# A two-layer graph-attention kernel: another order of the pieces where one batch hands over to the next, and edge masks loaded ahead of the source row

## The chip, the cores and the metric

The kernel runs on one core of a Trainium2 chip. The metric is the time of one launch on the device, in microseconds (us). A core has five engines with a queue of instructions each: TensorE (PE in the profile: matrix products; its weight loads are shown apart as PEld), VectorE (DVE), ScalarE (ACT), GpSimd (POOL) and SyncE (SP, which here only starts DMA transfers). They run side by side and wait for each other through semaphores.

## What is computed

x has 8 batches of 2048 nodes with 256 features; adj is a 2048 x 2048 mask of 0 and 1. Layer 0 is attention in four heads of 64, with a softmax of its own in each chunk of 256 keys, and layer 1 is a graph attention with additive scores. Each layer's output is added to its input and normalized. Cut to what matters:

```python
# layer 0
q, k, v = heads(x @ Wq.T + bq), heads(x @ Wk.T + bk), heads(x @ Wv.T + bv)
s = clip(q @ k.T / 8, -10, 10);  s = where(adj == 0, -10, s)
ctx = sum over chunks j of softmax(s[:, chunk j]) @ v[chunk j]
o = layernorm(ctx @ Wo.T + bo + x) * gamma + beta
x = layernorm(x + o)
# layer 1
Wh = x @ W
e = leaky_relu(s_src[:, None] + s_dst[None, :], 0.2), masked by adj
x = layernorm(x + elu(softmax(e) @ Wh))
```

## The kernel before

All 16 node tiles of 128 of one batch stay on the chip: `qT`, `kT` (features on the partitions), `vaug` (values and a column of ones, which gives the softmax sums) and `h1` (the output of layer 1). The 2048 query nodes are cut into four groups of 512, g = 0 to 3.

The order of each engine's instructions is the order in which the program writes them: scheduling is manual. The main loop over batches `b` has 64 slots `s`. A slot computes the scores of the next 512 queries by 256 keys for two heads (`scores`, L361), clips and masks them on VectorE (L382), takes exps on ScalarE (L394) and multiplies by the values (`product`, L396). `normalize` (L415) divides on GpSimd and adds to `acc`. Beside it runs layer 1 of the batch before (class `Layer1`): `make` (L689) builds a masked weight tile `e` on VectorE (L702) from a broadcast source row `srow`, a factor `gd` and the edge mask `et`, and `use` (L713) multiplies it by `waug` (L722). `tile_pool` buffers and PSUM tiles are handed on by semaphores; `two_banks` (L102) alternates between two PSUM tiles of two banks each, so a group of matmuls waits until the group two before it in that alternation was evicted.

Each 512-query group of layer 0 must, after its contexts are complete, go through: the output product (`Between.output`, L512), the add with x (L530), a norm (`a`), gamma and beta, a second add and norm (`b2`), the store of x1 (L546), a transposition, and the product with W (`values`, L554), whose results are the node values `waug` and the scores `sd` for layer 1. For groups 0 to 2 this is spread over the slots of the following group (tables `AHEAD`, `BESIDE`, `BEHIND`, `AFTER`). Group 3 has no slots after it. Its pieces are done between the last slot of one batch and the first slot of the next. With them go:

- the projections of the next batch, cut into pieces by `project` (L296): for each group g, `l` loads x, `t` transposes it on VectorE (L281), `k`, `v` and `q` are TensorE products (L315, L331) followed by an eviction on ScalarE (L323, L338). The piece `q3` takes PSUM tiles of another pool, and `l0` and `t0` are done earlier;
- `ctx`, the transposition of the last group's second half of contexts on TensorE (L454, evicted at L457), which needs the `acc` that GpSimd has just finished;
- `steps`, group 3's way to layer 1: 0 bias, 1 output product, 2 add, 3 shift and statistics of the first norm, 4 apply the first norm, 5 scale, second add and its statistics, 6 apply the second norm and store, 7 transposition of the eight blocks of y (`turn_all`, L290, evicted at L293), 8 and 9 the products with W (L565);
- `fs`, the three steps of `factors` (L604): the maximum of the destination scores, its spread with the exps, and the row: a transposed copy is stored to `rowD` in DRAM (L646) and scales `waug` on GpSimd (L649);
- `rest`, pieces of the closing work of layer 1's last unit (L744 to L758).

The list `order` in the program (L965 to L980) says in which order these pieces are written, and so fixes every engine's queue there. After it `Layer1(b, gd, waug)` is built, which issues the first loads on SyncE: the row (L673), which must come back from DRAM after the store at L646, and two edge tiles (L684), which come from masks stored at the start.

Of the kernel before, what the change touches and what calls it, by code (L numbers as in the profile page):

```python
# [22 lines left out]
def adj_resnorm_kernel(  # L23
# [170 lines left out]
    def send():  # L194
        while outgoing:
            outgoing.pop(0)()


    class Masks:
# [3 lines left out]
        def __init__(self):  # L203
            self.pieces = [(t, m) for t in range(NT) for m in range(len(BANKS))]
            self.raw, self.bits, self.done = [], [], []
            self.next = 0
# [148 lines left out]
    def load_slab(s):  # L355
        q, hp, c = where[s]
        slab = slabs.tile([P, KT, CH], I8, tag="slab", name="slab")
        nc.sync.dma_start(out=slab, in_=clipD[q][:, KT * c : KT * (c + 1), :])
        slab_of[s] = slab

    def scores(s):  # L361
        q, hp, c = where[s]
        slab = slab_of.pop(s)
        cols = slice(q * CH, (q + 1) * CH)
        pss = []
        for u in range(KT):
            t = KT * c + u
            ps = two_banks([P, 2, CH], "ps")
            for k in range(2):
                rows = slice(k * D, (k + 1) * D)  # L370
                nc.tensor.matmul(  # L371
                    ps[:, k, :],
                    lhsT=kT[rows, hp, t * P : (t + 1) * P],
                    rhs=qT[rows, hp, cols],
                    start=True,
                    stop=True,
                )
            pss.append(ps)
        probs[s] = []
        for u in range(KT):  # L380
            pr = prp.tile([P, 2, CH], F32, tag="pr", name="pr")
            nc.vector.scalar_tensor_tensor(  # L382
                pr,
                pss[u],
                -CLIP,
                slab[:, u, :].unsqueeze(1).to_broadcast([P, 2, CH]),
                op0=ALU.max,
                op1=ALU.min,
            )
            probs[s].append(pr)  # L390

    def exps(s, u):
        pr = probs[s][u]
        nc.scalar.activation(pr, pr, AF.Exp, scale=0.125)  # L394
# [46 lines left out]
    def load_context(b, q, hp):  # L441
        t = small.tile([P, 1, CH], F32, tag="ctx", name="ctx", bufs=1)
        load_squares(t, ctxD[b, q * CH : (q + 1) * CH, hp * P : (hp + 1) * P])
        sums[q, hp] = t

    def turn_context(q, hp):

        nc.vector.transpose(qT[:, hp, q * CH : (q + 1) * CH], sums.pop((q, hp))[:, 0, :])  # L448
# [209 lines left out]
    class Layer1:  # L658
        def __init__(self, b, gd, waug):
            self.b, self.gd, self.waug = b, gd, waug  # L660
            self.made = self.used = 0
            self.rows, self.edge, self.e = {}, {}, {}
            self.tail = []
            self.load_row(0)
            self.load_edge(0)
            self.load_edge(1)

        def load_row(self, n):
            if n < len(UNITS):
                m, h = UNITS[n]  # L670
                srow = small.tile([P, WIDE * P], F32, tag="srow", name="srow")
                i0, w = FIRST[m] * P, BANKS[m] * P
                nc.sync.dma_start(  # L673
                    out=srow[:, :w], in_=rowD[self.b, h, i0 : i0 + w].partition_broadcast(P)
                )
                self.rows[n] = srow
# [190 lines left out]
    for b in range(B):  # L867
        waug = blocks.tile([P, NT, H, D1], F32, tag="waug", name="waug")
        sd = small.tile([P, 2 * H, NT], F32, tag="sd", name="sd", bufs=1)
        if b == 0:  # L870
            for s in range(3):
                load_slab(s)
            scores(0)
            for u in range(KT):
                exps(0, u)
        if lower:
            for _ in range(STEP):
                lower.make()
        closing = Closing(b - 2, CLOSING) if b > 1 else None
        if closing:  # L880
            closing.do(-1)
        group = None
        for s in range(SLOTS):
            q, hp, c = where[s]
            i = s % QS
            send()
            if s + 3 < SLOTS:
                load_slab(s + 3)
            if i == 0:
                before = group  # L890
                group = Between(b, q - 1, sd, waug) if q else None
            if i == 1 and q:
                load_context(b, q - 1, 1)
            if i == QS // 2 + 1:
                load_context(b, q, 0)
            if group and i in AHEAD:
                AHEAD[i](group)
            if s == SLOTS - 3 and b + 1 < B:
                turns = [project(b + 1, g) for g in range(NCH)]
                turns[0].pop(0)()  # L900
            if s:
                normalize(s - 1)
            if s + 1 < SLOTS:
                scores(s + 1)

            if s == SLOTS - 1 and b + 1 < B:
                turns[0].pop(0)()
            if i == 3 and q:
                turn_context(q - 1, 1)
            if i == QS // 2 + 3:  # L910
                turn_context(q, 0)
            if group:
                for step in BESIDE.get(i, ()):
                    step(group)
            elif closing:
                closing.do(s, behind=False)
            product(s, 0, not lower)
            if s + 1 < SLOTS:
                for u in range(KT):
                    exps(s + 1, u)  # L920
            if lower:
                if b + 1 < B or s < SLOTS - LATE:
                    lower.step()
            elif masks.left():
                masks.step()
            product(s, 1, not lower)

            if before and i in AFTER:
                AFTER[i](before)
            if i == 0 and q:  # L930
                send_context(b, q - 1, 1)
            if i == QS // 2:
                send_context(b, q, 0)
            if group and i in BEHIND:
                BEHIND[i](group)
            elif closing and not q:
                closing.do(s, beside=False)
        normalize(SLOTS - 1)

        send()  # L940
        before = group
        gd, fs = factors(b, sd, waug)
        group = None
        every = tuple(range(QT))

        def begin():
            nonlocal group
            group = Between(b, NCH - 1, sd, waug)

        def ctx():  # L950
            context(NCH - 1, 1)

        steps = [
            lambda: group.bias(),
            lambda: group.output(every),
            lambda: group.add(every),
            lambda: (group.shift(), group.a.stats(every)),
            lambda: group.a.apply(group.y),
            lambda: (group.scale(), group.again(), group.b2.stats(every)),
            lambda: group.finish(),  # L960
            lambda: group.turn_all(),
            lambda: group.values((0, 1)),
            lambda: group.values((2, 3)),
        ]
        if b + 1 < B:  # L965
            (k0, v0, q0), (l1, t1, k1, v1, q1), (l2, t2, k2, v2, q2), (l3, t3, k3, v3, q3) = turns
            rest = [lambda: lower.rest(1)] if lower else []
            order = [begin, *rest, l1, *rest, lambda: before.values((2, 3)), *rest, k0, *rest, ctx]
            order += [v0, steps[0], t1, steps[1], k1, steps[2], q0, *steps[3:5], l2, v1, steps[5]]
            order += [steps[6], t2, q1, l3, k2, *steps[7:10], v2, fs[0], t3, q2, fs[1]]  # L970
            order += [lambda: [load_slab(s) for s in range(3)], k3, fs[2], v3]
            order += [lambda: scores(0), q3, lambda: [exps(0, u) for u in range(KT)]]
        else:

            step = lower.step
            order = [begin, lambda: before.values((2, 3)), steps[0], step, ctx, step, steps[1], step]
            order += [steps[2], step, steps[3], step, steps[4], step, steps[5], step, steps[6], step]
            order += [steps[7], step, steps[8], step, steps[9], step, fs[0], step, fs[1], step, fs[2]]
            order += [step, lambda: lower.rest(4)]
            assert sum(p is step for p in order) == LATE  # L980
        for piece in order:
            send()
            piece()
        send()
        lower = Layer1(b, gd, waug)
# [56 lines left out]
```

## Time and profile before

The median of 3 launches is 3862.64 us (3862.37 to 3863.09). The profiled launch spans 3861.0 us.

| Engine | Busy, us | Share of the span |
|---|---|---|
| TensorE, matrix products | 3687.8 | 96% |
| VectorE | 3204.6 | 83% |
| TensorE, weight loads | 2746.0 | 71% |
| ScalarE | 1953.6 | 51% |
| GpSimd | 1387.4 | 36% |

The mean granted clock of TensorE is 0.991 of full speed. A row of the page's groups names the line, the engine, the operation and its tiles, how often it ran, its busy time and mean duration, and the idle time of its engine just ahead of it with the releaser that ended most of it. In a timeline a row is one instruction or a run of like ones: start, duration, engine, line, operation, and in brackets the idle time ahead of it and what ended it. In a table of stretches each row has the length of the stretch, the busy time of each engine with its count of instructions, the granted TensorE clock, the DMA share and the GB/s moved.

### The profile page before, as it was taken

The numbers are of one execution on the slowest core, as the hardware profiler recorded it, in microseconds if no ns is written. First come the engines' busy times: TensorE is split into PE (matmuls) and PEld (weight loads), VectorE is DVE, ScalarE is ACT, GpSimd is POOL, SyncE is SP. The second block draws the span as 40 slices with busy tenths as digits, with TensorE's granted clock in tenths as the row PEclk, the third lists the DMA queues.
The fourth block names the chain that finished last, engine by engine and source line by source line (L and its number), as shares of the span: only waits on it lengthen the run. The fifth ranks groups of instructions, "written<-read, shape, count | busy, mean of one in ns | idle before, by whom it ended". The sixth has DMA issues, their size and how long they took to land. (4 is left out here: it accounts for less than half of the span.)

```text
span 3861.0 us, 160222 instructions
## 1 busy us (share of the span) xinstructions
PE 3687.8 (96%) x72068; PEld 2746.0 (71%) x72068; DVE 3204.6 (83%) x4810; ACT 1953.6 (51%) x3601; POOL 1387.4 (36%) x1202
## 2 busy tenths in 40 slices
PE   7999999999999999999999999999999999999787
PEld 4656677776777777776777767777677777776676
DVE  3877499986999779995999959998699977998798
ACT  3666445554555555554555545555455555555321
POOL 0445233332433333433433324343243333344310
PEclk9999999999999999999999999999999999999999
DMA  7642333333433333333433334333343433333344
GB/s 148 154 109 62 83 101 96 97 89 98 112 101 100 80 121 102 102 94 73 140 96 100 99 87 135 96 98 87 103 111 99 103 80 118 102 102 86 92 147 123
DMA packets 771328, 398.48 MB, mean 103 GB/s; under 512 B 442576, under 2 KB 735824, under 8 KB 770640
## 3 DMA queue, kind: packets, MB, share of 16 engines
q1 hardware_dynamic: 720640, 354.54, 36.3%
q10 hardware_dynamic: 50000, 33.70, 2.7%
q8 instruction: 563, 9.22, 1.0%
q14 instruction: 125, 1.02, 0.1%
HBM read 331.22 MB, written 56.89 MB: 101 GB/s over the span
## 5 line engine op out<-in xcount | busy, mean ns | idle before, releaser
L382 DVE SCALAR_TENSOR_TENSOR pr<-ps,slab 128x1024 f32<-128x1024 f32 x1024 | 1192.1, 1205 | 208.8 <-PE ps L371 206.7
L702 DVE SCALAR_TENSOR_TENSOR e<-srow,gd,et 128x640 f32<-128x640 f32 (+1 forms) x1536 | 1349.6, 934 | 17.9 <-DMA et<-edgeD 12.5
L406 PEld LDWEIGHTS pc<-vaug,pr 128*64 128x64 f32 x32768 | 1040.6, 138 | 445.5 <-issue 245.3
L406 PE MATMUL pc<-vaug,pr 128*64 128x65 f32 x32768 | 1157.9, 224 | 42.6 <-ACT raw L413 35.1
L394 ACT ACTIVATE pr<-pr 128x1024 f32<-128x1024 f32 x1024 | 1053.0, 1058 | 184.5 <-DVE pr L382 168.4
L722 PE MATMUL pa<-waug,e 128*64 128x65 f32 x32768 | 1081.5, 224 | 42.4 <-DVE e L702 40.0
L722 PEld LDWEIGHTS pa<-waug,e 128*64 128x64 f32 x32768 | 1020.1, 139 | 68.1 <-DVE e L702 39.8
L371 PE MATMUL ps<-qT,kT 64*128 64x512 f32 x4096 | 1027.4, 619 | 6.8 <-DVE pr L382 6.5
L428 POOL TENSOR_TENSOR part<-raw,rd 128x512 f32<-128x512 f32 x448 | 469.5, 1048 | 1462.1 <-DVE rd L421 1449.7
L413 ACT COPY raw<-pc 128x260 f32<-128x260 f32 x1024 | 384.9, 376 | 1157.7 <-PE pc L406 1132.2
L430 POOL TENSOR_TENSOR acc<-acc,part 128x512 f32<-128x512 f32 x448 | 574.9, 1283 | 35.1
L371 PEld LDWEIGHTS ps<-qT,kT 64*128 64x128 f32 x4096 | 351.3, 186 | 330.4 <-issue 209.7
L421 DVE RECIPROCAL rd<-raw 128x8 f32<-128x8 f32 x512 | 101.1, 197 | 116.7 <-ACT raw L413 113.0
L428 POOL TENSOR_TENSOR acc<-raw,rd 128x512 f32<-128x512 f32 x64 | 66.9, 1045 | 352.8 <-DVE rd L421 352.0
L750 ACT ACTIVATE hh<-pa,dn 128x64 f32<-128x64 f32 x512 | 114.4, 320 | 100.7 <-DVE dn L746 96.9
L315 PE MATMUL pp<-xT,wk_sb 128*128 128x512 f32 x256 | 124.1, 630 | 36.9 <-DVE xT L281 36.9
L565 PE MATMUL pw<-w_sb,x1T 128*128 128x264 f32 x512 | 138.7, 406 | 17.0 <-ACT x1T L293 9.0
L481 POOL TENSOR_TENSOR rs_c<-rs_c,nhalf 128x4 f32<-128x4 f32 x32 | 55.6, 1738 | 226.9 <-DVE off_c L480 226.9
L521 PE MATMUL po<-wo_sb,qT 128*128 128x256 f32 x512 | 125.5, 389 | 2.1 <-DVE qT L448 1.5
L315 PEld LDWEIGHTS pp<-xT,wk_sb 128*128 128x128 f32 x256 | 49.8, 200 | 94.3 <-issue 73.1
L315 PE MATMUL pp<-xT,wq_sb 128*128 128x512 f32 x256 | 116.0, 596 | 0.0
L331 PE MATMUL pv<-wv_sb,xT 128*128 128x256 f32 x512 | 115.9, 379 | 0.0
(90 smaller groups left out, 1885.1 us busy)
## 6 DMA issues: line engine op xcount, KB each, us to landing
et<-edgeD SPq DMA_DIRECT2D x256, 320.0 KB, 3.2
slab<-clipD SPq DMA_DIRECT2D x512, 128.0 KB, 3.6
et<-edgeD SPq DMA_DIRECT2D x128, 384.0 KB, 3.5
srow<-rowD SPq DMA_DIRECT2D x64, 320.0 KB, 4.4
xp<-in_x_dram SPq DMA_DIRECT2D x256, 64.0 KB, 2.3
xg<-in_x_dram SPq DMA_DIRECT2D x32, 512.0 KB, 4.7
x1D<-y ACTq DMA_DIRECT2D x32, 512.0 KB, 3.1
x1g<-x1D SPq DMA_DIRECT2D x32, 512.0 KB, 5.7
```

The lines of the kernel that those rows point to most:

```text
L315: nc.tensor.matmul(pps[c], lhsT=w[:, kc, c * P : (c + 1) * P], rhs=st["xT"][:, kc, :], start=(kc == 0), stop=(kc == KC - 1),)
L371: nc.tensor.matmul(ps[:, k, :], lhsT=kT[rows, hp, t * P : (t + 1) * P], rhs=qT[rows, hp, cols], start=True, stop=True,)
L382: nc.vector.scalar_tensor_tensor(pr, pss[u], -CLIP, slab[:, u, :].unsqueeze(1).to_broadcast([P, 2, CH]), op0=ALU.max, op1=ALU.min,)
L394: nc.scalar.activation(pr, pr, AF.Exp, scale=0.125)
L406: nc.tensor.matmul(pc[z * D : (z + 1) * D, i, :], lhsT=probs[s][u][:, k, i * P + z * D : i * P + (z + 1) * D], rhs=vaug[:, KT * c + u, 2 * ...
L413: nc.scalar.copy(raws[s][:, k], pc)
L428: nc.gpsimd.tensor_mul(part, raw[:, :, :, :D], rd.to_broadcast([P, 2, QT, D]))
L430: nc.gpsimd.tensor_add(accv, accv, part)
L521: nc.tensor.matmul(po[:, k, :], lhsT=qT[:, c, t * P : (t + 1) * P], rhs=wo_sb[:, c, :], start=(c == 0), stop=(c == KC - 1),)
L565: nc.tensor.matmul(pw[:, k, : F + 2 * H], lhsT=self.x1T[:, c, u * P : (u + 1) * P], rhs=w1_sb[:, c, :], start=(c == 0), stop=(c == KC - 1),)
L702: nc.vector.scalar_tensor_tensor(e[:, :w], self.rows[n][:, :w], self.gd[:, h, j : j + 1], self.edge[k // JG][:, j % JG, :w], op0=ALU.max, ...
L722: nc.tensor.matmul(self.pa[z * D : (z + 1) * D, i * D1 : (i + 1) * D1], lhsT=e[:, i * P + z * D : i * P + (z + 1) * D], rhs=self.waug[:, j ...
```

## The change

Two edits, no operation more or less. At the change of batches the pieces stand in another order: the contexts' transposition goes ahead of the first K projection, the output product ahead of the first V projection, the two applications of the norms ahead of the evictions of the Q projections next to them, and the transposition of y and the K projection of group 2 change places; the transposition of the last x group goes ahead of the maximum. The purpose is to start the longest dependent chain of this stretch (contexts, output product, two norms, transposition, products with W) earlier, and to have independent projections to run beside it. The last batch's branch is left as it was. In `Layer1`, the two edge tiles, which depend on nothing recent, are requested ahead of the row, whose request waits for its store.

```diff
             self.tail = []
-            self.load_row(0)
             self.load_edge(0)
             self.load_edge(1)
+            self.load_row(0)
...
             rest = [lambda: lower.rest(1)] if lower else []
-            order = [begin, *rest, l1, *rest, lambda: before.values((2, 3)), *rest, k0, *rest, ctx]
-            order += [v0, steps[0], t1, steps[1], k1, steps[2], q0, *steps[3:5], l2, v1, steps[5]]
-            order += [steps[6], t2, q1, l3, k2, *steps[7:10], v2, fs[0], t3, q2, fs[1]]
-            order += [lambda: [load_slab(s) for s in range(3)], k3, fs[2], v3]
+            order = [begin, *rest, l1, *rest, lambda: before.values((2, 3)), *rest, ctx, *rest, k0]
+            order += [steps[0], t1, steps[1], v0, steps[2], steps[3], l2, k1, steps[4], q0]
+            order += [steps[5], v1, t2, l3, steps[6], q1, steps[7], k2, steps[8], steps[9], t3, v2]
+            order += [lambda: [load_slab(s) for s in range(3)], fs[0], q2, fs[1], k3, fs[2], v3]
             order += [lambda: scores(0), q3, lambda: [exps(0, u) for u in range(KT)]]
```

## The prediction

> **What bounds the kernel now.** First the busy shares on the page, then who waited for whom over the whole run, then, since the diff touches only the change from one batch to the next (call it a junction; seven of the eight take the changed branch), the timeline of TensorE and of ScalarE through one junction, and last a table of stretches.
>
> ```profile
> PE 3687.8 (96%) x72068; PEld 2746.0 (71%) x72068; DVE 3204.6 (83%) x4810; ACT 1953.6 (51%) x3601; POOL 1387.4 (36%) x1202
> ```
>
> TensorE is the bound; only an idle piece of TensorE is worth anything. The list of waits:
>
> ```profile
> PE pp L315 <- DVE xT L281: 36.9, 11, 17.7
> ...
> PE pw L565 <- ACT x1T L293: 9.0, 7, 1.4
> ```
>
> Of the 36.9 us, 17.7 is the start of the program; the timeline has 2.44 us of it in each junction. The second line is 1.2 to 1.4 us in each of seven. TensorE in the junction from batch 2 to 3 (start, duration, what, idle before it):
>
> ```profile
> 1318.76 2.94 PE L565 MATMUL pw<-w_sb,x1T 128*128 128x264 f32 x12
> 1321.53 3.60 PE L315 MATMUL pp<-xT,wk_sb 128*128 128x512 f32 x8
> 1324.96 0.60 PE L454 MATMUL pt<-identf,acc 128*128 128x128 f32 x4
> ...
> 1328.86 3.62 PE L521 MATMUL po<-wo_sb,qT 128*128 128x256 f32 x16
> ...
> 1342.63 3.60 PE L315 MATMUL pp<-xT,wq_sb 128*128 128x512 f32 x8
> 1348.67 3.67 PE L315 MATMUL pp<-xT,wk_sb 128*128 128x512 f32 x8 [2.44 <-DVE xT L281]
> 1352.29 1.09 PE L290 MATMUL pt<-identf,y 128*128 128x128 f32 x8
> 1354.60 3.83 PE L565 MATMUL pw<-w_sb,x1T 128*128 128x264 f32 x16 [1.22 <-ACT x1T L293]
> 1358.26 3.62 PE L331 MATMUL pv<-wv_sb,xT 128*128 128x256 f32 x16
> ```
>
> The two gaps are all the idle time between 1321.53 and 1358.26. From start to start a K or Q projection takes 3.43, a V projection or output product 3.45, the context transposes 0.44, the eight transposes of y 0.98, the last values 3.66. These sum to 32.6 for k0, ctx, v0, output, k1, q0, v1, q1, k2, turn, values; the stretch took 36.73, so 4.13 us is lost: 2.61 ahead of k2, 0.19 in its slower first matmul, 1.33 ahead of the values. ScalarE there:
>
> ```profile
> 1340.53 2.07 ACT L486 ACTIVATE y<-y,off_a,rs_a 128x256 f32<-128x256 f32 x4
> ...
> 1348.45 2.08 ACT L486 ACTIVATE y<-y,off_b,rs_b 128x256 f32<-128x256 f32 x4 [4.61 <-POOL off_b L482]
> ...
> 1350.96 1.27 ACT L323 ACTIVATE qT<-pp,bq_sb 128x512 f32<-128x512 f32 x2 [0.44 <-ACT y L486]
> 1352.38 1.27 ACT L323 ACTIVATE kT<-pp,bk_sb 128x512 f32<-128x512 f32 x2
> 1353.53 1.01 ACT L293 COPY x1T<-pt 128x1024 f32<-128x1024 f32 x1
> ```
>
> The two norms are one chain, and t2 (the transposition that k2 needs) sits behind it on VectorE, although its data had long landed (in the junction before this one its load was issued by 870.6 and it ran at 887.8). The same stretch, k0 to v2, in all seven junctions (column PEclk is the granted clock):
>
> ```profile
> 405.35:442.08 36.73, 33.07 (x117) 20.84 (x116) 11.16 (x26) 15.10 (x26) 3.75 (x6) 1.00 0.32 64
> 862.10:900.53 38.43, 34.60 (x118) 21.52 (x117) 12.69 (x28) 15.82 (x28) 2.98 (x5) 0.96 0.29 58
> 1321.53:1358.26 36.73, 33.06 (x117) 20.84 (x116) 12.69 (x28) 15.82 (x28) 2.98 (x5) 1.00 0.29 59
> 1779.32:1817.75 38.43, 34.60 (x118) 21.51 (x116) 12.69 (x28) 15.81 (x28) 2.99 (x5) 0.96 0.28 56
> ...
> 3154.77:3193.19 38.42, 34.60 (x118) 21.49 (x116) 12.77 (x28) 15.81 (x28) 2.99 (x5) 0.96 0.31 62
> ```
>
> Three of seven took 1.70 us more, all with a lower clock: in each, the 3.41 us right after the 2.44 us gap ran at 0.50. The most that could be gained in the junctions is thus 7 x 4.13 + 3 x 1.70 = 34 us.
>
> [...]
>
> **The change part by part.** No operation is added or removed; TensorE's order becomes values, ctx, k0, output, v0, k1, q0, v1, q1, turn, k2, values, v2. Times are for the junction shown.
>
> *Context ahead of k0.* The transposes wait for acc, which GpSimd finishes at 1322.08 (1320.82 + 1.26), where TensorE was free at 1321.53: with 0.06 for the signal and up to 0.06 more, 0.67 us of new idle time on the path. k0, formerly here, hid it. In the first junction acc ends at 406.75 against 405.35, so it costs 1.46 there. Behind it everything is queued on TensorE.
>
> *Output ahead of v0.* Output starts at 1326.07 (ctx 1322.20 + 0.44 + 3.43), 2.8 earlier. Its add comes 3.65 after its start (1332.51 less 1328.86): 1329.72; the chain to off_a takes 4.35 on VectorE and 1.5 on GpSimd: 1335.4. The two-bank tiles alternate as before; each next group's bank was evicted over 1 us earlier, so v0 (1329.52), k1 (1332.97), q0 (1336.40), v1 (1339.83), q1 (1343.29) run without a gap, to 1346.72.
>
> *Norm ahead of q0's eviction.* ScalarE takes k1's eviction at 1336.60 and the first norm at 1337.75 instead of 1340.53. From there to the second norm is 7.92 as before (1348.45 less 1340.53): 1345.67 to 1347.75. q0's eviction follows the first norm at 1340.0, when its matmuls have just ended, so nothing is delayed.
>
> *The turn ahead of k2.* t2 comes at 1344.5 and is off the path. But the turn, free to start at 1346.72, waits for the last quarter of y at 1347.75 and ends near 1348.35 instead of 1347.70: 0.65 lost. k2 takes the bank of q1 now, and q1's eviction stands behind the second norm: 1347.75 + 0.43 + 1.27 = 1349.45. So k2 starts at 1349.5: 1.15 more, and 0.19 again for its first matmul. The eviction of x1T (to 1350.5) now lies beside k2, and the 1.33 ahead of the values go.
>
> Sum: 0.67 + 0.65 + 1.15 + 0.19 = 2.66 us instead of 4.13: 1.47 less, in six junctions, and 0.68 in the first: 9.5 us. From v2 on TensorE's order is unchanged and all that feeds it hangs on it, so the shift is kept.
>
> *t3 ahead of the maximum.* 1.25 us of VectorE in its 10.6 us of idle time: nothing.
>
> *The clock.* [...] I take the three half-rate windows as gone: 3 x 1.70 = 5.1 us. Ends: 0, or all seven at half rate, 4 x 1.70 = 6.8 lost.
>
> *Edges ahead of the row.* The first masks wait for edges 1.8 us in each junction:
>
> ```profile
> L702 DVE SCALAR_TENSOR_TENSOR e<-srow,gd,et 128x640 f32<-128x640 f32 (+1 forms) x1536 | 1349.6, 934 | 17.9 <-DMA et<-edgeD 12.5
> ```
>
> Edges now land some 15 us earlier; the row still waits for its store. VectorE gains up to 1.8 us there, but TensorE does not wait for these masks: its 0.48 us gap at 1381.46 is for exps behind q3's eviction on ScalarE, and it reaches the masks at 1382.33 without a gap. Worth nothing in seven junctions, and at the last one e follows h with no gap: nothing.
>
> Total 9.5 + 5.1 = 14.6: 3862.6 - 14.6 = 3848.0.
>
> **The rivals.** (1) As worked out: 3848.0; chance 0.50. (2) The half-rate windows remain in three junctions, [...]: 3853.1; 0.15. (3) They come in all seven: 3859.9, within 0.2%; 0.06. (4) q1's eviction does not hold k2 (another bank, or ScalarE through sooner): 1.15 more in seven, 3840; 0.17. For it: ScalarE is half idle; against it: the alternation puts q1 and k2 on one tile, and the turn already waited for q1's eviction in places in the trace before. (5) What is won in the junction is lost at the first slots to the row's round trip: about 3861; 0.07. Against it: the row's store hangs on the same TensorE order. (6) Slower: the norm does not come earlier, say because its add or ScalarE's queue is later than I think. The second norm stays at 1348.45, the turn then ends near 1351.1, q1's eviction at 1352.2, k2 follows, and v2 starts 1.3 later than before: 7 x 1.3 = 9 and 6.8 of half rate, 3878.5; 0.05. The profile speaks against it: from the output's end to the first norm ScalarE's only work is the evictions named.
>
> **How the numbers follow.** The prediction is case 1, 3848.0. Faster by over 0.2% (under 3854.9) are cases 1, 2 and 4: 0.82; the same, cases 3 and 5: 0.13; slower, 0.05. The range 3838 to 3858 holds 1, 2 and 4 with some 2 us at the low end for windows at half rate in the last batch's tail, and 5 us above case 2.
>
> **What would show it.** In the profile after: k0 to v2 spanning near 35.3 us in the later junctions; TensorE idle near 0.5 us before L454 (GpSimd acc), for L290 on y L486, and about 1.1 us before k2 on ScalarE's q eviction; no gap before L565; PEclk 1.00 in the stretch; the wait for et gone and replaced by a shorter one for the row. It is wrong if k2 starts straight behind the turn, if any junction is longer than 36.7 us, or if PEclk stays at 0.96 in several.

## The result, and the profile after

The median after is 3844.62 us (3842.80 to 3849.14, four launches) against 3862.86 us before on the same chip: a ratio of 0.9954, 95% interval 0.9937 to 0.9972. That is 18.2 us less; 14.6 were forecast. The engines on the page of the changed kernel:

```profile
PE 3692.3 (96%) x72068; PEld 2752.2 (72%) x72068; DVE 3203.3 (83%) x4810; ACT 1947.3 (51%) x3601; POOL 1385.4 (36%) x1202
```

TensorE is the bound as before, with the same 72068 matmuls. The timeline of TensorE in the junction from batch 2 to 3 (start, duration, what, idle before it and what ended it):

```profile
1318.09 2.94 PE L565 MATMUL pw<-w_sb,x1T 128*128 128x264 f32 x12
1321.47 0.66 PE L454 MATMUL pt<-identf,acc 128*128 128x128 f32 x4 [0.45 <-POOL acc L430]
1321.96 3.60 PE L315 MATMUL pp<-xT,wk_sb 128*128 128x512 f32 x8
1325.40 3.62 PE L521 MATMUL po<-wo_sb,qT 128*128 128x256 f32 x16
...
1342.62 3.60 PE L315 MATMUL pp<-xT,wq_sb 128*128 128x512 f32 x8
1346.06 0.42 PE L290 MATMUL pt<-identf,y 128*128 128x128 f32 x2
1346.64 0.33 PE L290 MATMUL pt<-identf,y 128*128 128x128 f32 x1 [0.16 <-ACT y L486]
1347.13 0.77 PE L290 MATMUL pt<-identf,y 128*128 128x128 f32 x5 [0.17 <-ACT y L486]
1348.84 3.70 PE L315 MATMUL pp<-xT,wk_sb 128*128 128x512 f32 x8 [0.94 <-ACT qT L323]
1352.38 3.72 PE L565 MATMUL pw<-w_sb,x1T 128*128 128x264 f32 x16
```

The two old waits (2.44 for t2, 1.22 for x1T) are gone. Three new ones stand in their place: for GpSimd's acc, for the quarters of y, and for q1's eviction. ScalarE shows why the last one is there:

```profile
1337.09 2.06 ACT L486 ACTIVATE y<-y,off_a,rs_a 128x256 f32<-128x256 f32 x4
...
1345.00 2.08 ACT L486 ACTIVATE y<-y,off_b,rs_b 128x256 f32<-128x256 f32 x4 [1.16 <-POOL off_b L482]
...
1347.52 1.26 ACT L323 ACTIVATE qT<-pp,bq_sb 128x512 f32<-128x512 f32 x2 [0.44 <-ACT y L486]
```

q1's matmuls end at 1346.2, but its eviction runs behind the second norm, from 1347.52 to 1348.78, and k2, which writes the same two banks, begins at 1348.84. The second norm stood ahead of q1's eviction before as well (at 1348.45 and 1350.96 there); of the two norms only the first has changed its place against an eviction of q. New is which group takes q1's banks: before it was the turn (the transposition of y), now it is k2. A table of stretches, from the last values ahead of the contexts (L565) to the third V projection (L331), for the first, second, third and last of the seven junctions; the granted clock is the third column from the right:

```profile
406.79:445.48 38.69, 36.19 (x130) 23.44 (x129) 12.85 (x29) 16.00 (x29) 5.59 (x6) 1.00 0.40 86
862.66:900.50 37.84, 36.13 (x133) 23.37 (x130) 13.14 (x31) 17.65 (x36) 4.73 (x6) 1.00 0.41 87
1318.09:1355.94 37.85, 36.13 (x133) 23.37 (x130) 13.12 (x31) 17.65 (x36) 4.74 (x6) 1.00 0.40 86
...
3140.26:3178.09 37.83, 36.12 (x132) 23.36 (x129) 13.11 (x31) 17.64 (x36) 4.74 (x6) 1.00 0.38 79
```

Before, the same stretches (by the starts of the same instructions) took 39.51 us, and 41.20 in the three with half clock. After, none has half clock. In what follows a junction is this stretch, and a loop is what lies between two junctions, from a batch's first product (L406) to the last values (L565) ahead of the next one's contexts. For the masks, the wait has changed its releaser:

```profile
L702 DVE SCALAR_TENSOR_TENSOR e<-srow,gd,et 128x640 f32<-128x640 f32 (+1 forms) x1536 | 1347.8, 933 | 12.3 <-PE pa L722 7.2 <-DMA srow<-rowD 5.0
```

The edges were last to land seven times for 12.5 us in all; now it is the row, in all seven again, for 5.0.

Where the 13.7 us between the two profiled spans (3861.0 and 3847.3) come from:

| Part of the launch | Change, us |
|---|---|
| Six junctions, each 39.51 to 37.85 at full clock | -10.0 |
| First junction, 39.51 to 38.70 | -0.8 |
| Three stretches at half clock that are gone, 1.70 each | -5.1 |
| The loops between junctions | -4.0 |
| Start of the launch to the first junction | +4.2 |
| From the last L565 ahead of the last contexts to the end | +2.1 |

The stretch from the third V projection to the batch's first product (L406) is 22.38 us in every junction of both. The start runs the same code in both and reached the first junction at 399.1 to 406.8 us in the ten kernels profiled here; the changed kernel's launch is the latest of them and had one stretch of 6.83 us there at half clock that before's had not. So the +4.2 is not the change's. Nor is the +2.1 shown to be: the end took 264.9 to 267.0 us in the ten kernels, and 265.1 both in the order alone and in the kernel that has one instruction more than the changed one. The other four rows add up to 19.9 us, near the 18.2 us of the medians.

### The profile page after: what moved, and what is told of

The parts are those of the page before. It is cut to its first block, busy times and chain, and to the rows that moved or that the text cites. A ratio compares the mean times of both kernels' runs of the same rounds, so it can differ in the third digit from the quotient of the medians.

```text
span 3847.3 us, 160215 instructions
## 1 busy us (share of the span) xinstructions
PE 3692.3 (96%) x72068; PEld 2752.2 (72%) x72068; DVE 3203.3 (83%) x4810; ACT 1947.3 (51%) x3601; POOL 1385.4 (36%) x1202
## 5 line engine op out<-in xcount | busy, mean ns | idle before, releaser
L382 DVE SCALAR_TENSOR_TENSOR pr<-ps,slab 128x1024 f32<-128x1024 f32 x1024 | 1192.1, 1205 | 214.0 <-PE ps L371 211.5
L406 PEld LDWEIGHTS pc<-vaug,pr 128*64 128x64 f32 x32768 | 1042.1, 138 | 440.9 <-issue 256.1
L406 PE MATMUL pc<-vaug,pr 128*64 128x65 f32 x32768 | 1159.4, 224 | 38.9 <-ACT raw L413 31.5
L722 PE MATMUL pa<-waug,e 128*64 128x65 f32 x32768 | 1084.6, 224 | 40.7 <-DVE e L702 39.1
L722 PEld LDWEIGHTS pa<-waug,e 128*64 128x64 f32 x32768 | 1024.1, 140 | 65.8 <-DVE e L702 39.8
L413 ACT COPY raw<-pc 128x260 f32<-128x260 f32 x1024 | 384.2, 376 | 1190.6 <-PE pc L406 1155.3
L565 PE MATMUL pw<-w_sb,x1T 128*128 128x264 f32 x512 | 138.1, 405 | 7.5 <-DVE x1T L281 7.4
L281 DVE STREAM_TRANSPOSE xT<-xp 128x1024 f32<-128x1024 f32 x32 | 39.5, 1235 | 102.0 <-PE pw L565 55.9
L331 PE MATMUL pv<-wv_sb,xT 128*128 128x256 f32 x512 | 115.9, 380 | 0.0
```

Source lines behind the costliest of these rows:

```text
L382: nc.vector.scalar_tensor_tensor(pr, pss[u], -CLIP, slab[:, u, :].unsqueeze(1).to_broadcast([P, 2, CH]), op0=ALU.max, op1=ALU.min,)
L406: nc.tensor.matmul(pc[z * D : (z + 1) * D, i, :], lhsT=probs[s][u][:, k, i * P + z * D : i * P + (z + 1) * D], rhs=vaug[:, KT * c + u, 2 * ...
L413: nc.scalar.copy(raws[s][:, k], pc)
L565: nc.tensor.matmul(pw[:, k, : F + 2 * H], lhsT=self.x1T[:, c, u * P : (u + 1) * P], rhs=w1_sb[:, c, :], start=(c == 0), stop=(c == KC - 1),)
L722: nc.tensor.matmul(self.pa[z * D : (z + 1) * D, i * D1 : (i + 1) * D1], lhsT=e[:, i * P + z * D : i * P + (z + 1) * D], rhs=self.waug[:, j ...
```

## The experiments

Each kernel is timed against before on its chip. The first edit is made to the kernel before, the others to the changed kernel unless the text says otherwise. The lengths of junctions and loops are taken from one profile each; junctions at full clock repeat to some hundredths of a us and loops to some tenths, which the whole time does not.

**Edges alone.**

```diff
-            self.load_row(0)
             self.load_edge(0)
             self.load_edge(1)
+            self.load_row(0)
```

> The order of pieces is that of before; only the two edge tiles are requested ahead of the row. The changed kernel's trace has the loops between the junctions (from the first product of a batch, L406, to the last values ahead of the next junction, L565) some 0.5 us shorter each, which the prediction had not. Theory (VectorE's lead lives on): the first masks start about 0.45 us earlier against TensorE and VectorE keeps that lead through slots in which it is the later one, so this kernel alone has those loops near 395.3 instead of 395.9 us, the junctions (L565 to the third V projection) unchanged at 39.5 and 41.2, and some 3.5 us less in all: 3859. Rival (the prediction's step, worth nothing): loops at 395.9, 3862.6 us within 0.5.

Measured 3858.40 us, 0.9984 (0.9977 to 0.9991): 6 us less than before on that chip. Loops of 395.3, 395.3, 395.6, 395.3 and 395.3 us where before had 395.9, 395.9, 396.3, 396.1 and 395.8; junctions at 39.50, or 41.20 and 41.05 in two with half clock. The edges alone are worth about 3 us in the loops. The forecast's "nothing" is refuted. The time's interval is 3.5 to 8.9 us less; of the 4.2 us between the two profiled launches, 1.9 come from the junctions, where this launch had one stretch at half clock fewer.

**The order alone.**

```diff
-            self.load_edge(0)
-            self.load_edge(1)
             self.load_row(0)
+            self.load_edge(0)
+            self.load_edge(1)
```

> The new order of pieces; the row is requested ahead of the edges as before. Theory: the junctions as in the changed kernel, 38.7 us in the first and 37.85 in the others, no stretch at half clock in any, loops back near 395.9: about 4 us slower than the changed kernel, 3848. Rival (the loops' gain comes from the order): loops near 395.3 and the same time as the changed kernel.

Measured 3846.99 us, 0.9956 (0.9941 to 0.9970). Junctions 38.68 and 37.84 to 37.85, no half clock; loops 395.8, 396.0, 396.0, 396.0, 396.2. So the order makes the junctions and the edges make the loops. The times (0.9956 and 0.9954) do not tell the order alone from both together; the loops do.

**q1 in other banks.**

```diff
-            lambda: linear(qT, wq_sb, bq_sb, b > 0 and g == NCH - 1),
+            lambda: linear(qT, wq_sb, bq_sb, b > 0 and g in (1, NCH - 1)),
```

> The changed kernel with q1's product in two single PSUM banks of the pool that q3 uses, so that k2 no longer takes the banks that q1's eviction holds. Theory (that eviction alone holds k2): the 0.94 us ahead of k2 go and nothing takes their place, junctions near 36.9 us, 7 x 0.94 = 6.6 us less in all: 3838. Rival (ScalarE is the bound of this piece): the values after k2 or the turn wait for ScalarE instead, under 2 us less in all.

Measured 3838.47 us, 0.9927 (0.9911 to 0.9944), junctions of 37.50 and then 36.65 to 36.66. TensorE in this kernel:

```profile
1343.43 0.77 PE L290 MATMUL pt<-identf,y 128*128 128x128 f32 x5 [0.16 <-ACT y L486]
1344.04 3.60 PE L315 MATMUL pp<-xT,wk_sb 128*128 128x512 f32 x8
1347.47 0.83 PE L565 MATMUL pw<-w_sb,x1T 128*128 128x264 f32 x3
```

k2 follows the turn with no gap, and no wait took its place: 1.19 us per junction, the 0.94 of the wait and the slower starts behind it. q1's eviction was what held k2. The interval of this time still overlaps that of the changed kernel, so the gain is read from the junctions.

**Contexts behind k0 again.**

```diff
-            order = [begin, *rest, l1, *rest, lambda: before.values((2, 3)), *rest, ctx, *rest, k0]
+            order = [begin, *rest, l1, *rest, lambda: before.values((2, 3)), *rest, k0, *rest, ctx]
```

> The changed kernel with the contexts' transposition behind k0 again, the output product still right behind it. Theory: GpSimd's 0.45 us go, but the output product waits for the contexts' eviction, which stands behind k0's two on ScalarE (1.27 + 0.59 us from 0.2 us after k0): it starts 1.5 us late, 0.9 us more per junction than in the changed kernel, near 38.7 us, about 6 us slower in all. Rival (the eviction runs beside, so that the early place only bought a wait for GpSimd): junctions near 37.3 us, 4 us faster.

Measured 3847.23 us, 0.9955 (0.9940 to 0.9970), junctions of 38.43 in all seven.

```profile
1320.33 0.60 PE L454 MATMUL pt<-identf,acc 128*128 128x128 f32 x4
1320.77 0.60 PE L521 MATMUL po<-wo_sb,qT 128*128 128x256 f32 x2
1322.33 3.29 PE L521 MATMUL po<-wo_sb,qT 128*128 128x256 f32 x14 [0.96 <-ACT qT L457]
```

GpSimd's wait is gone and the wait for the contexts' eviction is there, as the theory said, but it is smaller than worked out: the first two matmuls of the output product read the other half of the contexts and go ahead. It costs 0.58 us more per junction than the early place, in the first junction (where acc comes later) 0.27 less. The early place is right in six of seven. The times of the two kernels are not told apart.

**VectorE's lead, one instruction.** What the loops gain could be VectorE's earlier start or the transfers' other order.

```diff
+    pause = consts.tile([P, 400], F32, tag="pause", name="pause")
...
         if lower:
             for _ in range(STEP):
                 lower.make()
+            nc.vector.memset(pause, 0.0)
```

> The changed kernel with one more VectorE instruction in each batch from the second on: it sets a 128x400 tile that nothing reads to zero, right behind the first three masks and ahead of the scores' clipping, and so takes VectorE's 0.45 us of lead (0.2 to 0.5 us) away again, while every transfer stays as in the changed kernel. Theory (the lead is what the loops gained): the five loops from the third batch on go back toward 395.9 us, by as much as the instruction takes, the loop of the second batch stays at 394.8 (there is no closing work on VectorE there), junctions unchanged; about 2 to 3 us slower in all. Rival (the loops gained from the transfers, for example from edges that no longer compete with the slabs): the loops stay at 395.3.

Measured 3844.70 us, 0.9954 (0.9939 to 0.9969). The instruction took 0.39 us, yet three of the five loops stayed at 395.2; two took 395.7 and 395.6. Taken alone this is inconclusive, but the first mask, which waits for the row, does not start at the same place in each batch (2.90 to 3.78 us ahead of the first product in these five loops of the changed kernel), so the lead has to be read in each batch.

**VectorE's lead, three instructions.**

```diff
-            nc.vector.memset(pause, 0.0)
+            for _ in range(3):
+                nc.vector.memset(pause, 0.0)
```

> As the kernel with one extra VectorE instruction in each batch, but with three of them, 1.18 us. In that run the row happened to land early, so the scores' second clipping still began ahead of where before had it in three batches of five, and only the two batches where it began 0.2 us or more behind the first product had longer loops (395.6, 395.7 against 395.2). Theory (VectorE's place against TensorE at the start of the loop decides): now it begins 0.3 us or more behind the first product in every batch, as before, and all five loops from the third batch on take 395.6 to 396.2 us; the second batch's loop stays at 394.8 to 395.0. Rival (transfers, or chance): the loops stay spread between 395.2 and 395.7 as they were with one instruction.

Measured 3851.38 us, 0.9969 (0.9957 to 0.9980). All five loops became long. Worked out from the starts in the traces, for the loops of the third to seventh batch: the start of the second clipping of scores (VectorE, L382 and the same line of the other kernels) against the batch's first product (L406), and the length of the loop behind it:

```
before            +0.28 395.9   +0.34 395.9   +0.35 396.3   +0.50 396.1   +0.25 395.8
order alone       +0.30 395.8   +0.49 396.0   +0.50 396.0   +0.35 396.0   +0.66 396.2
edges alone       -0.40 395.3   -0.74 395.3   -0.69 395.6   -0.46 395.3   -0.62 395.3
changed           -0.74 395.2   -0.11 395.4   -0.31 395.4   -0.74 395.3   -0.74 395.2
one instruction   -0.41 395.2   -0.47 395.2   -0.28 395.2   +0.27 395.7   +0.22 395.6
three             +0.88 396.3   +0.47 395.9   +0.78 396.3   +0.61 396.1   +1.26 396.7
```

Ahead of the product 395.2 to 395.6, behind it 395.6 to 396.7, with the transfers' order of the changed kernel in the last two rows. So the start acts, and the transfers' order is not needed for it: at like starts (+0.47 with three instructions, +0.50 in before and in the order alone) the loops are alike, 395.9 and 396.0 to 396.1. The loop of the second batch, which has no closing work on VectorE, takes 394.8 to 395.0 in all six. How the lead acts some 80 us later, in before:

```profile
1456.53 2.19 ACT L394 ACTIVATE pr<-pr 128x1024 f32<-128x1024 f32 x2 [1.16 <-DVE pr L382]
...
1460.27 1.15 PE L406 MATMUL pc<-vaug,pr 128*64 128x65 f32 x32 [0.42 <-ACT raw L413]
```

And in the changed kernel, at the same place:

```profile
1453.72 2.19 ACT L394 ACTIVATE pr<-pr 128x1024 f32<-128x1024 f32 x2 [0.68 <-DVE pr L382]
...
1457.45 1.15 PE L406 MATMUL pc<-vaug,pr 128*64 128x65 f32 x32
```

VectorE, loaded with closing work, is late with the clipping; ScalarE waits for it with the exps and comes late to a later eviction (L413), and TensorE waits 0.42 us for that. With VectorE half a us earlier ScalarE's wait shrinks by as much and TensorE's is gone. Over the whole run the page shows the same, in before and in the changed kernel (the last number is TensorE's wait for the eviction at L413):

```profile
L406 PE MATMUL pc<-vaug,pr 128*64 128x65 f32 x32768 | 1157.9, 224 | 42.6 <-ACT raw L413 35.1
L406 PE MATMUL pc<-vaug,pr 128*64 128x65 f32 x32768 | 1159.4, 224 | 38.9 <-ACT raw L413 31.5
```

Summed from the traces over the five loops of the table, in us:

| Kernel | TensorE's waits for this eviction | The five loops |
|---|---|---|
| before | 21.1 | 1979.9 |
| order alone | 21.3 | 1979.9 |
| edges alone | 18.3 | 1976.6 |
| changed | 18.0 | 1976.5 |
| one instruction | 18.2 | 1977.0 |
| three | 22.2 | 1981.3 |

So of the 3.4 us that the loops of the changed kernel gained, 3.1 are this wait, and with three instructions it is back. It is not all that a loop's length depends on: the kernels with q1 apart or the contexts behind k0 have single loops of 395.6 to 396.1 with an early start. In two of these four TensorE has a new wait of another kind (0.82 us for a mask, 0.45 us of issue); the other two, the 396.1 among them, have hardly more idle time than the short loops and stay open.

**Contexts inside k0**, with q1 apart:

```diff
...
+                if c == 0 and mid:
+                    mid()
             for c in range(KC):
                 nc.scalar.activation(
...
-            order = [begin, *rest, l1, *rest, lambda: before.values((2, 3)), *rest, ctx, *rest, k0]
+            order = [begin, *rest, l1, *rest, lambda: before.values((2, 3)), *rest, *rest, lambda: k0(ctx)]
```

> The kernel with q1 apart, and the contexts' transposition between the two halves of k0's matmuls, its eviction ahead of k0's. Theory (the junction's losses are the waits for GpSimd and for ScalarE's evictions, each on its own): the wait for acc goes (0.62 us in six junctions, 1.4 in the first), the output product starts without a wait since the contexts' eviction ends some 0.9 us ahead of it; junctions near 36.05 us, some 5 us less than with q1 apart alone: 3833. Rival (the norm's chain, now nearer, takes it back at the turn): junctions stay near 36.6.

Measured 3831.83 us, 0.9919 (0.9905 to 0.9934), junctions of 35.97 to 35.98 in all seven, the first included.

```profile
1313.68 1.88 PE L315 MATMUL pp<-xT,wk_sb 128*128 128x512 f32 x4
1315.40 0.60 PE L456 MATMUL pt<-identf,acc 128*128 128x128 f32 x4
1315.84 1.88 PE L315 MATMUL pp<-xT,wk_sb 128*128 128x512 f32 x4
1317.56 3.62 PE L523 MATMUL po<-wo_sb,qT 128*128 128x256 f32 x16
```

Half of k0 covers GpSimd's addition and the other half the contexts' eviction; neither wait is left.

**Exps ahead of q3's eviction**, on top of that:

```diff
-            order += [lambda: scores(0), q3, lambda: [exps(0, u) for u in range(KT)]]
+            order += [lambda: scores(0), lambda: [exps(0, u) for u in range(KT)], q3]
```

> The kernel with the contexts inside k0 and q1 apart, and the first two exps of the next batch ahead of q3's eviction. Theory: the stretch from v2 to the first product, 22.38 us in every junction of every kernel so far, holds two waits for exps, 0.48 us and an issue gap of 0.76; they go, stretches near 21.5, some 6 us less: 3828. Rival (q3's eviction, now later, holds the new batch's layer 1 or scores in turn): the stretch shortens and the loop behind it grows by as much.

Measured 3828.64 us, 0.9914 (0.9898 to 0.9931). A miss: the stretch stays at 22.38, since the 0.76 us ahead of the first product is idle time of the weight loads alone; the scores' matmuls run on through it, here and ahead of later products. The 0.48 us lay behind that product's first matmuls and is gone, but the seven loops change by -0.67 to +0.45 us, 1.3 less in all, so most of it is given back there: TensorE's waits for exps fall from 5.7 to 2.3 us over the run, and those for the eviction of the products (L413 in the changed kernel) rise from 30.7 to 33.3. The two times do not tell this kernel from the one before it. Both are faster than the changed kernel: their intervals lie wholly below its own.

## Why the prediction was right

*Right.* The changed order's waits are those worked out, at the places named. The context's early place cost 0.61 us (start 3.38 after the values instead of 2.77) against 0.67 forecast. From q1's start to k2's it is 6.22 us; less the 3.43 + 0.98 that q1 and the turn take from start to start, 1.81 were lost against 0.65 + 1.15. The wait ahead of the values is gone. Rival 4 (q1's eviction does not hold k2) is refuted by the kernel with q1 apart, rival 6 by the second norm, which, counted from the values, came 2.78 us earlier (26.91 against 29.69), as forecast, and rival 5 by the 22.38 us that stayed. Rivals 2 and 3 fall with the half clock, below.

*Slips that cost nothing.* GpSimd's part of the chain to off_a is 1.3 us, not 1.5, and the 1335.4 holds with 1.3. t3 does not run in VectorE's idle time: it waits for the last values (11.47 us of idle time ahead of it, ended by PE pw L565) and so puts off the maximum by 0.9 us against v2; TensorE takes up the maximum only behind v2, so nothing was lost. "k0 to v2 near 35.3 us" is no measure of the new order, since the contexts now lie ahead of k0; counted from the end of the last values (2.77 us behind their start) it is 35.1 us.

*The size of the junction.* 1.47 us were forecast in six and 0.68 in the first; measured 1.66 and 0.81. The difference is small and not in one place: the context's wait is 0.06 less, its transposes take 0.05 more, k2's slow start is 0.08 less, the values are 0.10 shorter.

*The clock.* The forecast took three stretches at half clock as gone: they are. Before and the edges alone, with the old order, have 5 in 14 junctions; the eight kernels with the new order or more have none in 56. That they would go was the author's estimate; what decides between half and full clock was not shown. What the traces show is the time without other matmuls ahead of k2. In the kernel before it is 2.44 us, all of it idle, and half clock came in three of seven junctions. In the five kernels with the new order in which k2 still waits for q1's eviction, some 2.6 us lie between q1's last matmul and k2 that hold nothing but the eight transposes, and none of their 35 junctions was followed by half clock. In the changed kernel these are the 2.62 us from 1346.22 to 1348.84, in which TensorE was busy with transposes for 1.35 us.

*The step that failed* is "Edges ahead of the row ... Worth nothing in seven junctions". That the row becomes the last wait was right, and that TensorE does not wait for these first masks too. Wrong was to end there: VectorE has slots later in the batch in which it is the late one, and its earlier start is paid out there: 3.4 us in the six loops between junctions. (The loop ahead of the last contexts went from 380.5 to 379.9 us, but the edges alone had 380.7, so it is not counted.) This missing term and the 1.3 us in the junctions, 4.7 us, are a little more than the 3.6 us between forecast and result; the rest is within what launches differ by.

*Open.* The 6 us that the edges alone gained in the time are more than its loops show; the number of half-clock stretches differs between launches, and only one launch of each kernel was traced. Of the moves in the order only the contexts' was tried alone. Whether the turn should stand ahead of k2 was not: by the changed kernel's trace k2's input was ready at 1345.08 and the banks that it would take were free at 1343.84, so with k2 first the junction might have been about half a us shorter (an estimate from these starts and the 1.33 us that x1T cost before). By this estimate the gain comes from the earlier output product and norms, not from this exchange.

## What to carry to other kernels

When groups of matmuls that alternate between PSUM tiles change places, another group follows on each tile: look up which one, and where the eviction that it then waits for stands in the order of its engine; if that is late, give one of the two other banks. Here that was worth another 1.2 us per junction beside the 1.7 of the reordering. A wait on an engine that is off the path is worth nothing only if that engine is early everywhere behind it; look for the next place where it is the late one before writing zero (here the loops gained 3.4 us). And when a chain must wait for another engine, half of an independent group can be enough to cover it: here 1.72 us of k0 covered GpSimd's addition, the other 1.72 us the contexts' eviction, and six of the seven junctions went from 36.65 to 35.97 us.

## What was not expected of the hardware

The same wait was followed by half clock in some junctions and not in others. In the kernel before, TensorE has no matmul for 2.44 us ahead of k2 in every junction (2.45 in one). In three of the seven a stretch of 3.41 us with a granted clock of 0.50 began 0.15, 1.12 and 1.25 us after the end of that wait (at 889.39, 1807.58 and 3183.15), and the junction took 1.70 us more; in the other four the granted clock stayed at 1.00. So this 2.44 us gap cost 1.70 us more in three of seven; what sets them apart was not shown.

TensorE was not idle throughout ahead of such a stretch: in the 3.41 us ahead of the three it was busy for 0.97, 1.12 and 1.25 us. In the last batch's closing part, with smaller matmuls (128*64, L722), it was busy for 1.75 us in before and 1.61 us in the changed kernel in the 3.41 us ahead of 3650.78 and 3635.97, and 10.24 us at a granted clock of 0.50 followed in both.
